# Layer 1's attention with the context: a unit's value products by key block, with TensorE's order fixed

## The chip, the cores and the metric

The kernel runs on one core of one Trainium2 chip. A core has TensorE (matrix products), VectorE, ScalarE, GpSimd and SyncE, each with its own queue of instructions, and 16 DMA engines. The metric is the device time of one execution in microseconds (us). In the profile PE is TensorE, PEld its weight loads, DVE is VectorE, ACT is ScalarE, POOL is GpSimd and SP is SyncE.

## The reference

A decoder of two layers on 8 sequences of 512 tokens of 256 numbers, all in float32, each part followed by a layer norm of its sum with its input. Layer 0: self attention with decay, attention with the context, a feed-forward part with butterfly products. Layer 1: causal self attention, attention with the context, a mixture of experts. The change is in layer 1's attention with the context, where a query attends to its own 512 tokens and to the 64 of the context (8 heads of 64 numbers):

```python
    q1 = split_heads(x1 @ Wq1, N1)
    k1 = split_heads(x1 @ Wk1, N1)
    v1 = split_heads(x1 @ Wv1, N1)
    k2 = split_heads(x2 @ Wk2, N2)
    v2 = split_heads(x2 @ Wv2, N2)
    k = jnp.concatenate([k1, k2], axis=1)
    v = jnp.concatenate([v1, v2], axis=1)
    sim = jnp.einsum('bihd,bjhd->bhij', q1.astype(jnp.float32), k.astype(jnp.float32)) * scale
    attn = jax.nn.softmax(sim, axis=-1)
    out = jnp.einsum('bhij,bjhd->bihd', attn, v)
    out = out.reshape(B, N1, h * d)
    return out @ Wo + bo
```

Then the mixture of experts normalises each token, picks two of 8 experts by a router (softmax of a product with a 256 x 8 matrix, top two), and adds their weighted outputs.

## The kernel before

The kernel is one program of phases. Each phase is a list of units that go through the stages of a software pipeline (`_pipeline`): in step s, stage k works on unit s - k, and at the end of a step one piece of a list of postponed work (`put_off`) is run. A planner then sets the order of each engine's instructions: it takes them in the program's order as priority and lets one that is ready by its own estimate go ahead of one that isn't. It also adds the waits between engines.

In the phase "l1_context" a unit is (b, c, i): sequence b (8), head pair c (4), block i of 128 queries (4). So there are 128 steps, and "a unit's" four blocks i of one (b, c) share queries, keys and values. The stages are:

- `l1x_pre`, when i is 0: products for queries and keys of all 512 tokens (L953, tile s_qk), values (L960, t_v, kept in vc, two buffers); for a new b also the transposes of x and the context's values (L941, vx).
- `l1x_scores`, a step later: for each of the two heads j, one product with the 512 own keys (L980) and one with the 64 of the context (L981), both into one PSUM tile s_sc; VectorE takes the negated maximum (L982), ScalarE the exponential with its sum (L983); then the reciprocal of the sums (L840) and the scaling (L842).
- an empty stage.
- `l1x_transposes`: for each head four transposes of 128 x 128 (L279, tile tP) and a copy to SBUF (pt); then two transposes for the context's 64 keys (L995) and their copy (pt2). Copies alternate between VectorE (L94) and ScalarE (L96).
- `l1x_values`: for the 128 queries of block i, eight products (key block k, head j) of 64 output rows and 128 columns (L1007), and two with the context's values (L1016), all into 128 columns of the PSUM tile o_pv. After the last i the tile is copied to aT; after the last c the output projection (L225, o_out, in two pieces) and the norm go to `put_off`, and after them the router's four pieces: `route_norm`, `route_transposes` (L1075), `route_picks` (L1090 and some 20 small VectorE operations), `route_places` (L1129 to L1133, then eight scatters from GpSimd's queue).

PSUM holds two score tiles of two banks (s), two tiles for transposes (t) and two for outputs (o). A ring of eight 8 KB slots in SBUF holds weights; the phase uses four of them. The next phase, the experts, begins once all tokens are routed.

A product of float32 is issued as two matmul instructions, each with its weight load.

Of the kernel before, what the change touches and what calls it, by code (L numbers as in the profile page):

```python
# [11 lines left out]
F32 = mybir.dt.float32  # L12
# [6 lines left out]
P = 128  # L19
S = 512  # L20
D = 256
S2 = 64
NT = S // P
KC = D // P
NEG = -1.0e30
LN_EPS = 1e-5
SLOT = 2048
BLK = 256


def _pipeline(units, stages, later=None):


    units = list(units)
    for step in range(len(units) + len(stages) - 1):
        for k, stage in enumerate(stages):
            if 0 <= step - k < len(units):
                stage(*units[step - k])
        if later:
            later.pop(0)()  # L40
    while later:
        later.pop(0)()

# [2 lines left out]
def decoder_kernel(ctx: ExitStack, tc: tile.TileContext, a: dict, out: bass.AP):  # L46
# [8 lines left out]
    pe, act, dve, pool, sp = nc.tensor, nc.scalar, nc.vector, nc.gpsimd, nc.sync  # L55
# [34 lines left out]
    def evac(dst, src):  # L90

        n_evac[0] += 1
        if n_evac[0] % 2:
            dve.tensor_copy(dst, src)  # L94
        else:
            act.copy(dst, src)  # L96
# [18 lines left out]
    xs = [const.tile([P, NT, D], F32, name=f"x{b}") for b in range(NB)]  # L115
# [76 lines left out]
    def normed(dst, r, on_act=False):  # L192
# [52 lines left out]
    def pt_tile():  # L245
        return ph.tile([P, 2, NT, P], F32, tag="pt", name="pt")
# [27 lines left out]
    def probs_transposed(p, pt, n):  # L274

        for j in range(2):
            t = t_tile("tP")
            for k in range(n):
                pe.transpose(t[:, k, :], p[:, j, k * P : (k + 1) * P], ident)  # L279
            evac(pt[:, j, 0:n, :], t[:, 0:n, :])  # L280


    def butterfly_ops(bfly, bias_row, ahead=4):
# [58 lines left out]
    live = {}  # L342
# [191 lines left out]
    with tc.tile_pool(name="bfly", bufs=1, side="right") as bfly, phase("l0_self") as ph, psum("a", 3, 1, 1):  # L534
# [24 lines left out]
        units = [(b, g) for b in range(NB) for g in range(4)]  # L559
        later = []  # L560
# [43 lines left out]
        o = o_tile("o_bias")  # L604
# [14 lines left out]
    woT1 = slot("woT1").rearrange("p (c n) -> p c n", c=8)  # L619
# [107 lines left out]
    def big_tile(name, bufs=1):  # L727
        return ph.tile([P, 8, S], F32, tag="big", name=name, bufs=bufs)
# [115 lines left out]
    put_off = []  # L844
# [18 lines left out]

    def l1_transposes(b, c, i):
        pt = pt_tile()
        probs_transposed(live.pop(("p", b, c, i)), pt, i + 1)
# [8 lines left out]
    def out_done(b, c, w, n, plus, then=None):  # L875
        if c == 0:
            live["aT", b] = big_tile("aT")
        aT = live["aT", b]
        evac(aT[:, c, :], live.pop(("o", b, c)))
        if c == n - 1:  # L880
            project_and_norm(b, aT, w, n, plus(), put_off)
            if then:
                then(b)

    def l1_values(b, c, i):
        pt = live.pop(("pt", b, c, i))
        _, _, v = live["qkv", b, c]
        o = out_tile(b, c, i)
        for k in range(i + 1):
            for j in range(2):  # L890
                pe.matmul(  # L891
                    o[64 * j : 64 * (j + 1)],
                    lhsT=v[:, k, 64 * j : 64 * (j + 1)],
                    rhs=pt[:, j, k, :],
                    start=(k == 0),
                    stop=(k == i),
                )
        if i == NT - 1:
            out_done(b, c, woT1, 8, lambda: xs[b])

    with phase("l1_self") as ph:
        _pipeline(
# [14 lines left out]
    wo1 = v2_o[:, 1024:2048].rearrange("p (c n) -> p c n", c=4)  # L917
    for dst, name in ((wk2, "xa_wk2"), (wv2, "xa_wv2"), (wq1, "xa_wq1"), (wk1, "xa_wk1"), (wv1, "xa_wv1"), (wo1, "xa_wo")):
        sp.dma_start(out=dst, in_=rows(a[name]))
    NC2 = NB * S2  # L920
    k2 = slot("k2").rearrange("p (c n) -> p c n", c=4)
    for c in range(4):
        o = o_tile("o_k2")
        for kc in range(KC):
            pe.matmul(
                o[:, 0:NC2],
                lhsT=wk2[:, kc, c * P : (c + 1) * P],
                rhs=ctxT[:, kc, :],
                start=(kc == 0),
                stop=(kc == KC - 1),  # L930
            )
        evac(k2[:, c, 0:NC2], o[:, 0:NC2])

    def l1x_pre(b, c, i):
        if i:
            return
        if c == 0:
            xT = x_transposed(b)
            o = o_tile("o_v2")
            for kc in range(KC):  # L940
                pe.matmul(  # L941
                    o[0:S2, :], lhsT=ctxT[:, kc, b * S2 : (b + 1) * S2], rhs=wv2[:, kc, :], start=(kc == 0), stop=(kc == KC - 1)
                )
            vx = work.tile([P, S], F32, tag="lat", name="vx")
            evac(vx[0:S2, :], o[0:S2, :])
            live["xT", b], live["vx", b] = xT, vx
        xT = live["xT", b]
        cols = slice(c * P, (c + 1) * P)
        q, k = qk_tiles()
        s = s_tile("s_qk")  # L950
        for j, w in enumerate((wq1, wk1)):
            for kc in range(KC):
                pe.matmul(s[:, j, :], lhsT=w[:, kc, cols], rhs=xT[:, kc, :], start=(kc == 0), stop=(kc == KC - 1))  # L953

        act.mul(q, s[:, 0, :], 0.125)
        dve.tensor_copy(k, s[:, 1, :])
        t = t_tile("t_v")
        for j in range(NT):
            for kc in range(KC):
                pe.matmul(  # L960
                    t[:, j, :],
                    lhsT=xT[:, kc, j * P : (j + 1) * P],
                    rhs=wv1[:, kc, cols],
                    start=(kc == 0),
                    stop=(kc == KC - 1),
                )
        v = ph.tile([P, NT, P], F32, tag="vc", name="vc")
        act.copy(v, t)
        live["qkv", b, c] = q, k, v

# [16 lines left out]
        live["p", b, c, i] = p  # L987

    def l1x_transposes(b, c, i):
        p = live.pop(("p", b, c, i))  # L990
        pt = pt_tile()
        probs_transposed(p, pt, NT)
        t = t_tile("tP2")
        for j in range(2):
            pe.transpose(t[0:S2, j, :], p[:, j, S : S + S2], ident)  # L995
        pt2 = ph.tile([P, 2, P], F32, tag="pt2", name="pt2")
        evac(pt2[0:S2], t[0:S2, 0:2, :])
        live["pt", b, c, i] = pt, pt2

    def l1x_values(b, c, i):  # L1000
        pt, pt2 = live.pop(("pt", b, c, i))
        _, _, v = live["qkv", b, c]
        vx = live["vx", b]
        o = out_tile(b, c, i)
        for k in range(NT):
            for j in range(2):
                pe.matmul(  # L1007
                    o[64 * j : 64 * (j + 1)],
                    lhsT=v[:, k, 64 * j : 64 * (j + 1)],
                    rhs=pt[:, j, k, :],  # L1010
                    start=(k == 0),
                    stop=False,
                )
        for j in range(2):
            h = c * P + 64 * j
            pe.matmul(o[64 * j : 64 * (j + 1)], lhsT=vx[0:S2, h : h + 64], rhs=pt2[0:S2, j, :], start=False, stop=True)  # L1016
# [6 lines left out]
        if i == NT - 1:  # L1023
            out_done(b, c, wo1, 4, plus, routed)


    gb = keep.tile([P, 2, KC], F32, name="gb")
# [134 lines left out]

    ph = ctx.enter_context(phase("l1_experts"))
# [135 lines left out]
    for b in range(NB):  # L1299
        t = ph.tile([P, NT, D], F32, tag="last", name="last", bufs=4)  # L1300
# [95 lines left out]
```

## Time and profile before

| | |
|---|---|
| three runs | 4045.73, 4053.77, 4060.9 us; median 4053.77 |
| the profiled execution | 4058.26 us, its span 4056.5 us, mean granted clock 0.947 |
| 0 to 971 us | layer 0's self attention |
| 971 to 1412 us | layer 0's attention with the context, its feed-forward part, and the start of layer 1 |
| 1412 to 2417 us | layer 1's self attention |
| 2417 to 3385 us | layer 1's attention with the context, router pieces between |
| 3385 to 3442 us | the last sequence's projection, norm and routing |
| 3442 to 4056.5 us | the experts and the last norm |

The stages are read from the timeline; their borders overlap by a few us. Busy times count the union of an engine's instructions; the end of a matmul in the trace is modelled, so intervals between starts say more than durations. "Idle before" is the time an engine stood still ahead of an instruction, and the name behind the arrow is what ended it.

### The profile page before, as it was taken

The page shows a single profiled execution, that of the slowest core. Times are in us where ns is not written, and L with a number is a line of the kernel's source. Part 1 is how long each engine was busy: PE and PEld are TensorE (multiplying, and loading weights), DVE is VectorE, ACT ScalarE, POOL GpSimd, SP SyncE. Part 2 cuts the span into 40 slices and gives each one's busy share as a digit, 9 for nine tenths or more (in the row PEclk, how much of TensorE's full clock was granted, in tenths as well). Part 3 has the DMA queues.
Part 4 walks back from the last instruction along what each step waited for, and adds up shares of the span by engine and source line. Part 5 has one row for each costly group of instructions (what it writes and reads, how often), then busy time and mean ns, then how long its engine had stood idle before and what let it go on. Part 6 is the DMA issues. An engine that isn't in the chain of part 4 may idle for free. (4 is left out here: it accounts for less than half of the span.)

```text
span 4056.5 us, 58011 instructions
## 1 busy us (share of the span) xinstructions
PE 3799.6 (94%) x22164; PEld 2393.7 (59%) x22164; DVE 2195.0 (54%) x6177; ACT 1418.2 (35%) x2980; POOL 1098.8 (27%) x974
## 2 busy tenths in 40 slices
PE   8999999998999999999999999999999995999995
PEld 3333333346656655666566665666666664888884
DVE  5666656558942377777777765555555553000002
ACT  2443343442221254444544433333333331222222
POOL 4767566652211122211211110110101101122222
PEclk8999899997789999999999999999999997999997
DMA  3000011119500122222322220000000001766664
GB/s 120 25 22 22 22 32 32 32 52 236 124 6 1 32 37 32 32 32 32 40 35 32 32 32 1 17 13 10 12 17 17 17 11 40 243 183 182 182 183 107
DMA packets 173432, 236.12 MB, mean 58 GB/s; under 512 B 26554, under 2 KB 138618, under 8 KB 173155
## 3 DMA queue, kind: packets, MB, share of 16 engines
q1 hardware_dynamic: 146562, 179.93, 14.6%
q0 software_dynamic: 26592, 52.49, 9.0%
q8 instruction: 175, 2.87, 0.3%
q14 instruction: 103, 0.84, 0.1%
HBM read 136.78 MB, written 62.03 MB: 49 GB/s over the span
## 5 line engine op out<-in xcount | busy, mean ns | idle before, releaser
L417 DVE CUSTOM_DVE_ANT_0 scored<-s_sc,decay 128x512 f32<-128x512 f32 x512 | 323.4, 687 | 293.4 <-PE s_sc L412 291.9
L470 ACT ACTIVATE pt<-s_st 128x1024 f32<-128x1024 f32 x256 | 261.4, 1024 | 373.0 <-PE o_pv L481 224.9
L810 POOL DMA_DIRECT2D qk<-turned x256 | 202.6, 1207 | 627.0 <-issue 273.0
L96 ACT COPY pt<-tP 128x128 f32<-128x128 f32 (+2 forms) x480 | 224.3, 467 | 384.2 <-PE tP L279 299.2
L279 PE MATMUL tP<-ident,p 128*128 128x128 f32 x2304 | 355.5, 287 | 2.3 <-DVE pt L94 0.8
L279 PEld LDWEIGHTS tP<-ident,p 128*128 128x128 f32 x2304 | 250.6, 143 | 145.8 <-issue 74.0
L269 ACT ACTIVATE p<-p,nm 128x128 f32<-128x128 f32 (+3 forms) x512 | 283.0, 555 | 145.4 <-DVE nm L267 145.4
L983 ACT ACTIVATE p<-s_sc,nm 128x576 f32<-128x576 f32 x256 | 189.6, 743 | 348.9 <-DVE nm L982 348.9
L1287 DVE TENSOR_SCALAR y<-o_y,share 128x256 f32<-128x256 f32 x78 | 34.2, 479 | 491.8 <-PE o_y L1265 491.8
L842 DVE TENSOR_SCALAR p<-p,rsum 128x576 f32<-128x576 f32 (+4 forms) x768 | 295.4, 428 | 6.1
L1249 PE MATMUL s_h<-xnT,we 128*128 128x256 f32 x1248 | 284.7, 381 | 2.8 <-DMA we<-in_mo_w 2.8
L412 PE MATMUL s_sc<-k,q 32*128 32x512 f32 x1024 | 267.5, 703 | 16.4 <-ACT k L398 14.0
L94 DVE COPY pt<-tP 128x128 f32<-128x128 f32 (+2 forms) x480 | 259.1, 540 | 42.5 <-PE tP L279 28.6
L257 DVE CUSTOM_DVE_ANT_0 p<-s_sc,tabs 128x128 f32<-128x128 f32 (+3 forms) x512 | 234.9, 484 | 84.9 <-PE s_sc L855 84.9
L855 PE MATMUL s_sc<-qk 64*128 64x128 f32 (+3 forms) x1024 | 265.8, 486 | 12.3 <-DVE turned L807 8.2
L1265 PE MATMUL o_y<-we,h 128*128 128x256 f32 x1248 | 275.6, 379 | 0.0
L1265 PEld LDWEIGHTS o_y<-we,h 128*128 128x128 f32 x1248 | 237.1, 190 | 32.2
L1249 PEld LDWEIGHTS s_h<-xnT,we 128*128 128x128 f32 x1248 | 232.6, 191 | 32.2 <-DMA we<-in_mo_w 3.2
L982 DVE TENSOR_REDUCE nm<-s_sc 128x1 f32<-128x576 f32 x256 | 183.6, 749 | 119.1 <-PE s_sc L981 119.1
L1288 POOL DMA_INDIRECT total<-y,to x78 | 121.2, 1554 | 458.5 <-DVE y L1287 295.1
L891 PE MATMUL o_pv<-pt,vc 128*64 128x128 f32 x2560 | 221.8, 284 | 0.0
L1007 PE MATMUL o_pv<-pt,vc 128*64 128x128 f32 x2048 | 197.7, 287 | 0.0
(248 smaller groups left out, 6476.1 us busy)
## 6 DMA issues: line engine op xcount, KB each, us to landing
we<-in_mo_w SPq DMA_DIRECT2D x78, 1024.0 KB, 5.7
rows_in<-zero SPq DMA_DIRECT2D x64, 530.0 KB, 11.2
qk<-turned POOLq DMA_DIRECT2D x256, 128.0 KB, 4.4
xr<-rows_in SPq DMA_DIRECT2D x39, 265.0 KB, 6.2
coef<-in_ff_upw SPq DMA_DIRECT2D x40, 256.0 KB, 3.2
coef<-in_ff_dnw SPq DMA_DIRECT2D x40, 256.0 KB, 3.1
x<-in_x SPq DMA_DIRECT2D x8, 512.0 KB, 9.4
total<-x SPq DMA_DIRECT2D x8, 512.0 KB, 2.9
```

The lines of the kernel that those rows point to most:

```text
L94: dve.tensor_copy(dst, src)
L96: act.copy(dst, src)
L257: dve.tensor_tensor_reduce(out=p[:, j, 0:n], in0=s[:, j, 0:n], in1=m, scale=1.0, scalar=-3.0e38, op0=op, op1=reduced, accum_out=mx[:, j : ...
L269: act.activation(p[:, j, 0:n], p[:, j, 0:n], AF.Exp, bias=nm[:, j : j + 1], scale=scale, accum_out=sums[:, at + j : at + j + 1],)
L279: pe.transpose(t[:, k, :], p[:, j, k * P : (k + 1) * P], ident)
L412: pe.matmul(s[:, j, :], lhsT=q[h : h + 32, i * P : (i + 1) * P], rhs=k[h : h + 32, :], start=True, stop=True)
L417: dve.tensor_tensor_reduce(out=scored[:, h, :], in0=s[:, j, :], in1=decay[:, i, :], scale=1.0, scalar=-3.0e38, op0=ALU.mult, op1=ALU.max, ...
L470: act.activation(pt, s, AF.Exp, scale=1.0 / 16.0)
L842: dve.tensor_scalar(p[:, j, 0:n], p[:, j, 0:n], rsum[:, j : j + 1], None, ALU.mult)
L855: pe.matmul(s[:, j, 0:n], lhsT=q[h : h + 64, i * P : (i + 1) * P], rhs=k[h : h + 64, 0:n], start=True, stop=True)
L1249: pe.matmul(s[:, j, :], lhsT=w1[:, c, f * P : (f + 1) * P], rhs=xnT[:, c, :], start=(c == 0), stop=(c == KC - 1),)
L1265: pe.matmul(o[:, i, :], lhsT=h[:, f, i * P : (i + 1) * P], rhs=w2[:, f, :], start=(f == 0), stop=(f == 7),)
```

## The change

Stages now carry their own delay, and they are listed in the order in which a step issues them: `l1x_pre` (0), `l1x_scores` (1), `l1x_transposes` (3), `l1x_values` (7), `l1x_last_transposes` (3). The probabilities of all four query blocks of a unit are collected transposed in two SBUF tiles of 512 columns, one for each head, in two sets by the parity of c. While the transposes of the next unit run, `l1x_values` makes one product over all 512 queries for one key block k and each head in each of four steps, and in the fourth also the two products of the context. The context's transposes stand behind the values. Within the phase TensorE takes its instructions in the program's order. Each router piece has an empty step ahead of it. vc has three buffers.

```diff
-def _pipeline(units, stages, later=None):
+def _pipeline(units, stages, later=None, pieces=1):
...
     units = list(units)
-    for step in range(len(units) + len(stages) - 1):
-        for k, stage in enumerate(stages):
+    stages = [s if isinstance(s, tuple) else (k, s) for k, s in enumerate(stages)]
+    for step in range(len(units) + max(k for k, _ in stages)):
+        for k, stage in stages:
             if 0 <= step - k < len(units):
                 stage(*units[step - k])
-        if later:
-            later.pop(0)()
+        for _ in range(pieces):
+            if later:
+                later.pop(0)()
...
-            evac(pt[:, j, 0:n, :], t[:, 0:n, :])
+            evac(pt[j], t[:, 0:n, :])
...
+    pts = [[slot("pt").rearrange("p (k n) -> p k n", k=NT) for _ in range(2)] for _ in range(2)]
...
-        v = ph.tile([P, NT, P], F32, tag="vc", name="vc")
+        v = ph.tile([P, NT, P], F32, tag="vc", name="vc", bufs=3)
...
     def l1x_transposes(b, c, i):
+        p = live["p", b, c, i]
+        if i == 0:
+            live["pt", b, c] = pts[c % 2], ph.tile([P, 2, S], F32, tag="pt2", name="pt2")
+        pt, _ = live["pt", b, c]
+        probs_transposed(p, [pt[j][:, :, i * P : (i + 1) * P] for j in range(2)], NT)
+
+    def l1x_last_transposes(b, c, i):
+
         p = live.pop(("p", b, c, i))
-        pt = pt_tile()
-        probs_transposed(p, pt, NT)
+        _, pt2 = live["pt", b, c]
         t = t_tile("tP2")
         for j in range(2):
             pe.transpose(t[0:S2, j, :], p[:, j, S : S + S2], ident)
-        pt2 = ph.tile([P, 2, P], F32, tag="pt2", name="pt2")
-        evac(pt2[0:S2], t[0:S2, 0:2, :])
-        live["pt", b, c, i] = pt, pt2
-
-    def l1x_values(b, c, i):
-        pt, pt2 = live.pop(("pt", b, c, i))
+        evac(pt2[0:S2, :, i * P : (i + 1) * P], t[0:S2, 0:2, :])
+
+    def l1x_values(b, c, k):
+
+        if k == 0:
+            live["o", b, c] = o_tile("o_pv")
+        o = live["o", b, c]
+        pt, pt2 = live["pt", b, c]
         _, _, v = live["qkv", b, c]
         vx = live["vx", b]
-        o = out_tile(b, c, i)
-        for k in range(NT):
-            for j in range(2):
-                pe.matmul(
-                    o[64 * j : 64 * (j + 1)],
-                    lhsT=v[:, k, 64 * j : 64 * (j + 1)],
-                    rhs=pt[:, j, k, :],
-                    start=(k == 0),
-                    stop=False,
-                )
+        for j in range(2):
+            pe.matmul(
+                o[64 * j : 64 * (j + 1)], lhsT=v[:, k, 64 * j : 64 * (j + 1)], rhs=pt[j][:, k, :], start=(k == 0), stop=False
+            )
+        if k < NT - 1:
+            return
         for j in range(2):
             h = c * P + 64 * j
             pe.matmul(o[64 * j : 64 * (j + 1)], lhsT=vx[0:S2, h : h + 64], rhs=pt2[0:S2, j, :], start=False, stop=True)
...
     def routed(b):
-        put_off.extend(partial(f, b) for f in (route_norm, route_transposes, route_picks, route_places))
-
-    with phase("l1_context") as ph:
+
+        for f in (route_norm, route_transposes, route_picks, route_places):
+            put_off.extend((nothing, partial(f, b)))
+
+    with phase("l1_context") as ph, tc.manual_schedule(engines={PE}):
         _pipeline(
             [(b, c, i) for b in range(NB) for c in range(4) for i in range(NT)],
-            [l1x_pre, l1x_scores, nothing, l1x_transposes, l1x_values],
+            [(0, l1x_pre), (1, l1x_scores), (3, l1x_transposes), (7, l1x_values), (3, l1x_last_transposes)],
             put_off,
         )
```

More of the change, by code (lines that the diff above doesn't have):

```diff
@@ L26 @@
 LN_EPS = 1e-5
+PE = mybir.EngineType.PE
 SLOT = 2048
 BLK = 256
-def _pipeline(units, stages, later=None):
+def _pipeline(units, stages, later=None, pieces=1):
     units = list(units)
-    for step in range(len(units) + len(stages) - 1):
-        for k, stage in enumerate(stages):
+    stages = [s if isinstance(s, tuple) else (k, s) for k, s in enumerate(stages)]
+    for step in range(len(units) + max(k for k, _ in stages)):
+        for k, stage in stages:
             if 0 <= step - k < len(units):
                 stage(*units[step - k])
-        if later:
-            later.pop(0)()
+        for _ in range(pieces):
+            if later:
+                later.pop(0)()
     while later:
@@ L865, in l1_transposes @@
         pt = pt_tile()
-        probs_transposed(live.pop(("p", b, c, i)), pt, i + 1)
+        probs_transposed(live.pop(("p", b, c, i)), [pt[:, j, 0 : i + 1, :] for j in range(2)], i + 1)
         live["pt", b, c, i] = pt
@@ L873, in out_tile, with out_done @@
         return live["o", b, c][:, i * P : (i + 1) * P]
-    def out_done(b, c, w, n, plus, then=None):
+    def out_done(b, c, o, w, n, plus, then=None):
         if c == 0:
@@ L878, in out_done @@
         aT = live["aT", b]
-        evac(aT[:, c, :], live.pop(("o", b, c)))
+        evac(aT[:, c, :], o)
         if c == n - 1:
@@ L898, in l1_values @@
         if i == NT - 1:
-            out_done(b, c, woT1, 8, lambda: xs[b])
+            out_done(b, c, live.pop(("o", b, c)), woT1, 8, lambda: xs[b])
     with phase("l1_self") as ph:
@@ L1021, in plus @@
             return xb
-        if i == NT - 1:
-            out_done(b, c, wo1, 4, plus, routed)
+        out_done(b, c, o, wo1, 4, plus, routed)
     gb = keep.tile([P, 2, KC], F32, name="gb")
```

## The prediction

> **What bounds the kernel now.** I read the page first, then the busy time by stage, then the timeline of one steady step of the changed stage, TensorE alone and then the engines that empty PSUM.
>
> ```profile
> PE 3799.6 (94%) x22164; PEld 2393.7 (59%) x22164; DVE 2195.0 (54%) x6177; ACT 1418.2 (35%) x2980; POOL 1098.8 (27%) x974
> ```
>
> ```profile
> core 0: us, PE busy (x) PEld busy (x) DVE busy (x) ACT busy (x) POOL busy (x), PEclk, DMA share, GB/s
> ...
> 2417.00:3385.00 968.00, 909.33 (x6329) 608.94 (x6327) 551.89 (x1302) 345.22 (x818) 84.43 (x77) 0.96 0.04 13
> ```
>
> The changed stage runs from 2417 to 3385 us. TensorE is busy 94% of it, VectorE 57%, ScalarE 36%, and DMA hardly at all. A unit (batch b, head pair c) has four steps, so there are 128 steps. A plain step takes 4.69 or 4.98 us by turns, mean 4.835. This is one of the longer ones, on TensorE:
>
> ```profile
> 2905.18 1.14 PE L980 MATMUL s_sc<-k,q 64*128 64x512 f32 x4
> 2906.14 0.34 PE L981 MATMUL s_sc<-k,q 64*128 64x64 f32 x4
> 2906.41 1.09 PE L279 MATMUL tP<-ident,p 128*128 128x128 f32 x8
> 2907.43 0.65 PE L1007 MATMUL o_pv<-pt,vc 128*64 128x128 f32 x6
> 2908.65 0.41 PE L995 MATMUL tP<-ident,p 128*64 128x128 f32 x2 [0.57 <-ACT pt L96]
> 2908.99 0.87 PE L1007 MATMUL o_pv<-pt,vc 128*64 128x128 f32 x10
> 2909.79 0.43 PE L1016 MATMUL o_pv<-pt,vx 64*64 64x128 f32 x4
> 2910.16 1.14 PE L980 MATMUL s_sc<-k,q 64*128 64x512 f32 x4
> ```
>
> From start to start: scores 1.23, transposes 1.02, values 1.22 (with the idle 0.57), the context's transposes 0.34, values 0.80, the context's values 0.37: 4.98. The other kind of step idles 0.27 in the same place. So a step has 4.41 us of work and 0.42 of idle time on average. The idle time ends with a copy out of PSUM, since there are only two transpose buffers and a step needs three. The engines that make those copies:
>
> ```profile
> 2906.50 1.42 DVE L982 TENSOR_REDUCE nm<-s_sc 128x1 f32<-128x576 f32 x2 [0.83 <-PE s_sc L981]
> 2907.30 0.74 ACT L983 ACTIVATE p<-s_sc,nm 128x576 f32<-128x576 f32 x1 [2.66 <-DVE nm L982]
> ...
> 2907.84 0.68 DVE L94 COPY pt<-tP 128x512 f32<-128x512 f32 x1
> ...
> 2908.03 0.58 ACT L96 COPY pt<-tP 128x512 f32<-128x512 f32 x1
> 2908.49 0.76 ACT L983 ACTIVATE p<-s_sc,nm 128x576 f32<-128x576 f32 x1
> ...
> 2909.37 0.17 DVE L840 RECIPROCAL rsum<-sums 128x2 f32<-128x2 f32 x1 [0.84 <-ACT p L983]
> 2909.57 0.95 DVE L842 TENSOR_SCALAR p<-p,rsum 128x576 f32<-128x576 f32 x2
> ```
>
> VectorE's step is 1.42 (maxima) + 0.68 (a copy) + 0.17 + 0.95 + 0.20 (the small copy every other step) = 3.42 us. The copy at 2907.84 stands behind both maxima.
>
> The change's price depends on whether products of different columns of the array run abreast when they are 512 wide. The stage itself has them only 128 wide, so I looked at layer 0, and for one undivided product at L953:
>
> ```profile
> 804.68 1.07 PE L481 MATMUL o_pv<-pt,vaug 128*32 128x512 f32 x8
> 805.68 0.73 PE L412 MATMUL s_sc<-k,q 32*128 32x512 f32 x4
> ...
> 2890.09 3.70 PE L953 MATMUL s_qk<-xT,q_k 128*128 128x512 f32 x8
> 2893.62 1.95 PE L960 MATMUL t_v<-v_k,xT 128*128 128x128 f32 x16
> ```
>
> Every float32 product is issued as two instructions. Undivided ones take 0.44 us each at 512 columns (3.53/8). The eight of L481, four column tiles by two, take 1.00 us to the next group's start, so four run abreast.
>
> **What the Trainium skill says.** "TensorEngine Tiling", Key Properties: tiles work in parallel, and changing the tiling mode drains TensorE. The trace agrees: four abreast above, and 1.00 us where two passes alone are 0.88. "TensorE: Matmul & The Clock Gate", Part 1 (engine queue depths): VectorE and ScalarE take their queues in strict order; the copy behind the maxima shows it. The same part says that TensorE's clock halves after idle windows. The trace has a mean of 0.96 here, with dips after the router's 8-wide products; these stay.
>
> **The change, part by part.**
>
> *Values.* Before, a step's 8 value products (16 instructions) are cut by the planner as 10 and 6 or 6 and 10, an odd number of products each, so that one of each part runs unpaired. Work: (1.22 - 0.57) + 0.80 = 1.45, and 0.37 for the context, 1.82 a step. After, a step has two products of 512 columns, one pair abreast: 1.00 us as L481, its mode change included. Each unit's fourth step adds the context pair, 1.00 again. Columns streamed are equal; what goes is the unpaired slots and mode changes. Not shown is a pair of 64 columns at 512. Bounds: 1.00 (abreast), 0.88 + 0.88 + 0.10 = 1.86 (one after the other). I take 1.00, since 64-column pairs at 128 columns and 32-column groups at 512 both run abreast.
>
> *Work of a step after.* 1.23 + 1.02 + 1.00 + 0.34 = 3.59, in the fourth 4.59; mean 3.84, against 4.41.
>
> *Idle time after.* TensorE's order is now scores, transposes, values, the context's transposes. I put the copies where the trace has them, counted from the end of the scores. A step whose first copy is on ScalarE: maxima 0.09 to 1.51, first exponential to 1.63, first copy to 2.20, second exponential to 2.84. One whose first copy is on VectorE: copy 1.43 to 2.11, second exponential done at 2.35, scaling to 3.62, small copy to 3.95. TensorE is ready for the third transpose at 2.02 and gets its buffer at about 2.2: idle 0.15 to 0.24. The fourth step (3.02) waits for nothing. Queued behind that wait are the next scores, and behind these both maxima. The next scores start at 2.51 to 2.6, but their second half needs the bank that the second exponential frees, in the ScalarE kind of step at about 2.96 (2.84, and 0.12 because VectorE came late from the small copy). So one kind of step takes 2.51 + 1.23 = 3.74, the other about 3.0 + 1.23 = 4.25; mean 4.0, fourth step 4.6; over a unit 4.15. VectorE's 3.42 fits, with 0.7 to spare where it had 1.4.
> Gain: (4.835 - 4.15) x 128 = 88 us.
>
> *Start and end.* Values run three steps further behind. At the end four value groups and the context's stand alone (5.0 us) where one step's stood (about 1.5): +3.5. At the start three more steps run without values, at VectorE's pace rather than TensorE's; and the first transposes can't be drawn ahead of the stage (six of eight are at 2405.8 now): about +1.5. Together -5.
>
> *Router pieces.* The same instructions, with an empty step before each, three steps later in the batch. VectorE's normalisation and picks come to about 14 us a batch, TensorE's products to 6.5. SP's store and POOL's eight scatters move along; only the last batch's are waited for, in the tail from 3385 to 3442, which stays. The fixed order adds a real wait: the transposes (L1075), L1090 and L1129 stand in TensorE's queue, and everything behind them waits for VectorE. In the unloaded tail the normalisation takes 8 us (3392.3 to 3400.4) and the picks 4.3 (3406.6 to 3410.9). Loaded, there are 22 us for the first (four steps and one projection of 5.3), which mostly covers it, and 8.3 for the second, with VectorE 0.7 free in each step. Bounds: 0 and 5 us a batch; I take 1.75, 14 us in all.
>
> *At nothing.* Value buffers taken from the ring (four slots that only the next stage needs, after 3442), a third vc buffer, wider pt2: no engine time. The copies have the same sizes, with another stride.
>
> Sum: 88 - 5 - 14 = 69 us. The profiled execution took 4058.3 (span 4056.5); 4058.3 - 69 = 3989. The runs' median is 4.5 us lower, so I forecast 3985.
>
> **Rivals.**
> *TensorE alone sets the pace* (no idle time: the planner puts copies ahead of maxima where it helps): 3.84 a step, 127 - 5 = 122, 3932. For it: VectorE and ScalarE have room on average. Against: two transpose buffers and two score buffers stay.
> *The softmax loop sets it*, scores to maxima to exponential to the next scores, at about 4.45 a step because a copy falls into it: 49 - 5 - 20, 4030. For it: the second exponential is already behind a copy in half of the steps.
> *TensorE held at the router, slower*: the fixed order keeps scores behind L1075, L1090 and L1129, whose inputs VectorE delivers late since it is now 85% busy in a plain step. It decides from (88 - 5)/8 = 10.4 us of waiting a batch. At 13 us, 4075. Against: the 22 us of lead.
> *The pair doesn't run abreast*: steps of 4.45, fourth 6.31, mean 4.92: +11 + 5 + 14, 4084.
>
> **How the numbers follow.** About 0.5% (20 us) can be told from no change. My forecast 0.58 (its own range 3955 to 4015), TensorE alone 0.14, softmax loop 0.14, held at the router 0.10, not abreast 0.04. Half of the softmax loop's falls within 0.5%, and a little of the router's. Faster 0.79, same 0.08, slower 0.13. The range takes in the first rival and the softmax loop's upper side: 3935 to 4050.
>
> **What would show it.** Right: value products of 512 columns starting in pairs a few ns apart, a group about 1.0 us; plain steps near 4.0 and 4.6; idle time before L995's transposes down from 0.42 to about 0.15; the stage some 70 us shorter. Wrong: values at 1.8 us a group; idle time of several us before L1075, L1090 or L1129; scores waiting for the exponential in every step; or a clock well under 0.96 in the stage.

## The result, and the profile after

The changed kernel takes 3995.78 us (median of 4 runs, 3987.99 to 3997.32) against 4052.96 us of the kernel before: ratio 0.985, 95% interval 0.9833 to 0.9868. The forecast was 3985 us, 0.3% lower. The profiled execution took 3987.99 us, the shortest of the four, with a span of 3986.3 us where the kernel before had 4056.5. So the two traces differ by 70 us, the medians by 57.

First the busy times and the two stages, from the page and from the view of busy time by stretch (columns as in the prediction; the first row is layer 1's attention with the context, the second the last sequence's projection and routing):

```profile
PE 3727.7 (94%) x20244; PEld 2264.5 (57%) x20244; DVE 2191.8 (55%) x6177; ACT 1418.0 (36%) x2980; POOL 1097.8 (28%) x974
```

```profile
2412.00:3313.00 901.00, 845.32 (x4407) 489.68 (x4405) 551.89 (x1301) 345.92 (x818) 81.09 (x74) 0.96 0.04 13
3313.00:3379.00 66.00, 21.04 (x91) 17.84 (x90) 18.56 (x85) 4.61 (x7) 13.42 (x14) 0.59 0.17 60
```

TensorE has 1920 instructions fewer, which is 128 steps times 15. The stage has shrunk from 968 to 901 us, and of these 67 us 64 are TensorE's busy time (909.33 to 845.32). VectorE's busy time in it is the same to 0.01 us. The tail, from the stage's last value product to the experts' first product, was 64 us before and is 66. So what was gained was gained in the stage that was changed, and as work of TensorE. The rest of the 70 us of the span is 5.5 us by which the stage begins earlier, in phases that the change doesn't touch (in the traces of this study it begins anywhere between 2407 and 2423 us).

The timeline of TensorE, two steps (start, duration, engine, line, operation, tiles, shapes, count; then the idle time before and what ended it):

```profile
2882.05 0.41 PE L1008 MATMUL tP<-ident,p 128*64 128x128 f32 x2 [0.20 <-ACT pt L100]
2882.39 1.52 PE L986 MATMUL s_sc<-k,q 64*128 64x512 f32 x4
2883.35 0.72 PE L987 MATMUL s_sc<-k,q 64*128 64x64 f32 x4
2884.00 1.09 PE L283 MATMUL tP<-ident,p 128*128 128x128 f32 x8
2885.02 1.08 PE L1020 MATMUL o_pv<-pt,vc 128*64 128x512 f32 x4
2886.03 0.41 PE L1008 MATMUL tP<-ident,p 128*64 128x128 f32 x2
2886.37 1.14 PE L986 MATMUL s_sc<-k,q 64*128 64x512 f32 x4
2887.33 0.34 PE L987 MATMUL s_sc<-k,q 64*128 64x64 f32 x4
2887.61 1.09 PE L283 MATMUL tP<-ident,p 128*128 128x128 f32 x8
2888.63 1.08 PE L1020 MATMUL o_pv<-pt,vc 128*64 128x512 f32 x4
2889.64 1.08 PE L1027 MATMUL o_pv<-pt,vx 64*64 64x512 f32 x4
2890.64 0.41 PE L1008 MATMUL tP<-ident,p 128*64 128x128 f32 x2
```

From start to start the four instructions of L1020 take 1.01 us, and the context's (L1027) 1.00. The first step is 3.98 us; its scores take 1.61 where the second step's take 1.24, because their second half waits for a score buffer. The second step is a unit's fourth.

What TensorE waits for in the stage (engine, tile and line, what ended the wait: us in total, times, longest):

```profile
PE tP L1008 <- ACT pt L100: 21.0, 52, 1.6
PE tP L1008 <- DVE pt L98: 13.1, 11, 2.4
...
PE o_rank L1139 <- DVE both L1129: 6.1, 7, 1.2
```

and before:

```profile
PE tP L995 <- ACT pt L96: 29.5, 54, 0.6
PE tP L995 <- DVE pt L94: 21.8, 49, 3.3
```

The wait for a transpose buffer, 51.3 us before, is still the largest, with 34.1. The router's ranks hold TensorE for 6.1 us in all.

### The profile page after: what moved, and what is told of

It reads as the page before. It is cut to its first block, busy times and chain, and to the rows that moved or that the text cites. A ratio compares the mean times of both kernels' runs of the same rounds, so it can differ in the third digit from the quotient of the medians.

```text
span 3986.3 us, 54132 instructions
## 1 busy us (share of the span) xinstructions
PE 3727.7 (94%) x20244; PEld 2264.5 (57%) x20244; DVE 2191.8 (55%) x6177; ACT 1418.0 (36%) x2980; POOL 1097.8 (28%) x974
## 5 line engine op out<-in xcount | busy, mean ns | idle before, releaser
L989 ACT ACTIVATE p<-s_sc,nm 128x576 f32<-128x576 f32 x256 | 189.5, 742 | 291.5 <-DVE nm L988 253.1
L416 PE MATMUL s_sc<-k,q 32*128 32x512 f32 x1024 | 266.6, 699 | 16.4 <-ACT k L402 14.0
L895 PE MATMUL o_pv<-pt,vc 128*64 128x128 f32 x2560 | 221.8, 284 | 0.0
L1155 POOL DMA_INDIRECT rows_in<-z,irow x64 | 63.1, 985 | 475.0 <-DVE hit L1150 347.6
## 6 DMA issues: line engine op xcount, KB each, us to landing
rows_in<-zero SPq DMA_DIRECT2D x64, 530.0 KB, 10.2
```

The costliest lines, as they stand in the source:

```text
L416: pe.matmul(s[:, j, :], lhsT=q[h : h + 32, i * P : (i + 1) * P], rhs=k[h : h + 32, :], start=True, stop=True)
L989: act.activation(p[:, j, :], s[:, 0 : S + S2], AF.Exp, bias=nm[:, j : j + 1], accum_out=sums[:, j : j + 1])
```

## The experiments

All kernels compute the whole of the reference. Below, "the change" is the changed kernel, "narrow" values are those of the kernel before (128 columns, ten small products a step), "wide" ones those of the change. Ratios are to the kernel before in the same session, with their 95% interval.

**Part one: which part of the change brings the gain.** Four variants of the change, each with one part undone. In the first the planner orders TensorE again:

```diff
-    with phase("l1_context") as ph, tc.manual_schedule(engines={PE}):
+    with phase("l1_context") as ph:
```

> The changed kernel, with TensorE's order in this phase left to the planner again. Theory A (the gain is in the step's work: whole pairs and fewer mode changes): in this shape the planner's order differs from the program's in few places, mostly at the start and beside the router, so 3985 to 4005 us. Theory B (the fixed order brings the gain): back near 4050.

Measured: 3987.9 us, 0.9824 (0.9806 to 0.9842); the stage is 901.2 us long, the change's 900.8. Fixing the order brings nothing. (TensorE stands idle for 33.7 us in it instead of 55.7, but its scores take 207.1 us from start to start instead of 194.3: where one head's half of the scores waits while the other's runs, TensorE isn't idle.)

In the second the router's pieces come in successive steps, as before the change:

```diff
-            put_off.extend((nothing, partial(f, b)))
+            put_off.append(partial(f, b))
```

> The changed kernel, with the router's pieces in successive steps, without the empty step ahead of each. Theory A, as in the prediction: with TensorE's order fixed, TensorE meets the router's products before VectorE has made their inputs, about 4 us more of waiting a batch at the normalised tokens' transposes and at the rank products: 4020 to 4040. Rival (VectorE catches up in any case, the empty steps do nothing): 3990 to 4000.

Measured: 4037.05 us, 0.9947 (0.9933 to 0.9961): two thirds of the gain are gone. The views of waits and of busy time by stretch of this kernel:

```profile
PE o_rank L1139 <- DVE both L1129: 19.8, 7, 3.1
```

```profile
2460.00:3340.00 880.00, 815.34 (x4110) 476.86 (x4108) 519.40 (x1222) 321.01 (x758) 80.83 (x73) 0.92 0.04 13
```

and the change's own row over about as much work (4171 matmul instructions against 4110):

```profile
2460.00:3300.00 840.00, 790.35 (x4171) 460.37 (x4168) 520.81 (x1235) 324.89 (x772) 75.74 (x68) 0.96 0.04 13
```

The wait for the picks is 19.8 us instead of 6.1, a mean of 2.8 over seven batches instead of 0.9. More is lost in another way: the stage is 54 us longer (955.2 to 900.8, by the starts on TensorE), its idle time only 18 (74.0 to 55.7). The other 36 are work at a lower clock: 0.92 in the stretch instead of 0.96. The trace's record of the granted clock, which has only full and half speed in this stage, gives 157 us at half speed against 75; idle time left out, that costs some 38 us. The empty steps are therefore worth two things, a shorter wait and a higher clock.

In the third the values are narrow again, one step after the transposes, with the fixed order, the context's transposes still behind the values and the router still apart (vc has two buffers again):

```diff
-            [(0, l1x_pre), (1, l1x_scores), (3, l1x_transposes), (7, l1x_values), (3, l1x_last_transposes)],
+            [(0, l1x_pre), (1, l1x_scores), (3, l1x_transposes), (4, l1x_values), (3, l1x_last_transposes)],
...
     def l1x_transposes(b, c, i):
+        pt = pt_tile()
+        probs_transposed(live["p", b, c, i], pt, NT)
+        live["pt", b, c, i] = pt
...
+    def l1x_values(b, c, i):
+        pt, pt2 = live.pop(("pt", b, c, i))
```

> The values in the old shape (eight products of 128 columns and two of the context for one block of queries, one step after the transposes), but with TensorE's order fixed, the context's transposes behind the values, and the router's pieces apart. Theory A (whole pairs, and the third transpose's wait covered by the values): work 1.23 + 1.02 + 1.03 + 0.37 + 0.34 = 3.99 us a step, mean about 4.06 with idle time, so 3975 to 4000, no slower than the wide form. Theory C (the 512-wide products themselves bring it): 4030 to 4055.

Measured: 3964.25 us, 0.977 (0.9754 to 0.9787). This was the surprise of the study: without the wide products the kernel is about 0.8% *faster* than with them. Its timeline of one step, and two of its groups (instructions, busy us, mean ns, idle before):

```profile
2896.21 1.09 PE L281 MATMUL tP<-ident,p 128*128 128x128 f32 x8
2897.23 1.09 PE L1013 MATMUL o_pv<-pt,vc 128*64 128x128 f32 x16
2898.26 0.44 PE L1022 MATMUL o_pv<-pt,vx 64*64 64x128 f32 x4
2898.62 0.41 PE L1001 MATMUL tP<-ident,p 128*64 128x128 f32 x2
```

```profile
L1013 PE MATMUL o_pv<-pt,vc 128*64 128x128 f32 x1920 | 135.3, 285 | 0.0
...
L1001 PE MATMUL tP<-ident,p 128*64 128x128 f32 x238 | 48.6, 286 | 16.0 <-ACT pt L98 9.6 <-DVE pt L96 6.3
```

against the change's:

```profile
L1020 PE MATMUL o_pv<-pt,vc 128*64 128x512 f32 x484 | 132.2, 625 | 0.0
...
L1008 PE MATMUL tP<-ident,p 128*64 128x128 f32 x242 | 49.6, 287 | 31.9 <-ACT pt L100 18.8 <-DVE pt L98 12.0
```

The sixteen small instructions stand together and take 1.03 us, the four large ones 1.01. So the 1.45 us that a step's own values cost before weren't the price of small products: it was that of products cut by the planner into parts of ten and six instructions, five and three products, each with one that has no partner.

The starts of the single instructions in the two traces say what this costs. Two that run abreast start 6 or 7 ns apart, and the next pair, or the next that is alone, 109 ns later. Sixteen together are eight pairs. Of ten, eight are paired and two alone, of six, four are paired and two alone: ten slots for eight, 0.22 us. From start to start the parts take 0.80 and 0.58 us, 1.38 in all (the other 0.07 of the 1.45 is already the wait). So 0.14 us of the difference to 1.03 is left for the second change of kind. In the stage before, 508 of the 2048 instructions start alone, here none.

The narrow form has 0.36 us of the context's values in every step, the wide one 1.00 in every fourth.

In the fourth the values are wide, but the two products of a step belong to the same head, so that neither has a partner on the other half of the columns:

```diff
-        for j in range(2):
+        j = k // 2
+        for kk in (2 * (k % 2), 2 * (k % 2) + 1):
             pe.matmul(
-                o[64 * j : 64 * (j + 1)], lhsT=v[:, k, 64 * j : 64 * (j + 1)], rhs=pt[j][:, k, :], start=(k == 0), stop=False
+                o[64 * j : 64 * (j + 1)], lhsT=v[:, kk, 64 * j : 64 * (j + 1)], rhs=pt[j][:, kk, :], start=(kk == 0), stop=False
             )
```

> The changed kernel, but the two products of a step belong to one head (two key blocks of head 0 in the first and second step, of head 1 in the third and fourth), so the same columns of the array and no pair; the number and size of products is unchanged. Theory A (pairs run abreast): a group takes 1.86 instead of 1.00 us, the wait for the third transpose goes, +0.55 us a step, 4055 to 4075. Theory C (width is what counts): 3990 to 4000.

Measured: 4035.6 us, 0.9949 (0.9936 to 0.9963), some 40 us more than the change. Its timeline:

```profile
2892.11 1.93 PE L1021 MATMUL o_pv<-pt,vc 128*64 128x512 f32 x4
2893.97 0.41 PE L1008 MATMUL tP<-ident,p 128*64 128x128 f32 x2
```

The group takes 1.86 us, the upper bound of the prediction, and 0.85 us more than a pair: 109 us over 128 steps. Only 40 of these show, since the longer group covers waits: only 2.9 us of idle time follow the values here (31.9 in the change), and the scores, whose second half no longer waits, take 181.5 us in the stage instead of 194.3.

**Part two: where the narrow form's gain comes from.** Three more kernels: narrow values as in the third above but with the planner's order; the same with the fixed order and the context's transposes ahead of the values; and the kernel before with an empty step ahead of each router piece, nothing else changed.

```diff
-    with phase("l1_context") as ph, tc.manual_schedule(engines={PE}):
+    with phase("l1_context") as ph:
```

> The kernel of e3 (narrow values, the context's transposes behind them, router pieces apart) with TensorE's order left to the planner. Theory A (what counts is the order in which the program lists the work, and that pairs stay whole; the fixing itself is not needed where the planner keeps that order): 3955 to 3985. Theory B (the fixed order itself): 4030 or more.

Measured: 3966.37 us, 0.9769 (0.9755 to 0.9784).

```diff
-            [(0, l1x_pre), (1, l1x_scores), (3, l1x_transposes), (4, l1x_values), (3, l1x_last_transposes)],
+            [(0, l1x_pre), (1, l1x_scores), (3, l1x_transposes), (3, l1x_last_transposes), (4, l1x_values)],
```

> The kernel of e3 with one thing moved: the context's transposes ahead of the values, as the kernel before lists them, in the fixed order. Theory A: the third transpose waits for the first copy, about 1.15 us after TensorE is ready, with nothing to cover it and the whole queue behind it: step 5.1 against 4.06, 4070 to 4105. Rival (another wait of the step shrinks by as much, so this one is hidden anyway): below 4000.

Measured: 4106.91 us, 1.0113 (1.0097 to 1.0128), slower than the kernel before. The timeline shows why:

```profile
2895.84 1.09 PE L281 MATMUL tP<-ident,p 128*128 128x128 f32 x8
2898.09 0.41 PE L1001 MATMUL tP<-ident,p 128*64 128x128 f32 x2 [1.16 <-ACT pt L98]
2898.43 0.77 PE L1013 MATMUL o_pv<-pt,vc 128*64 128x128 f32 x10
```

The third pair of transposes needs the buffer of the first, whose copy comes about 2.2 us after the transposes began. With nothing between them TensorE stands 1.16 us here, 135 us in the stage; with the values between, nothing in the step shown above and 16 us in the stage. The planner of the kernel before got around this by putting ten or six of the sixteen instructions between, and paid with the unpaired ones. So this one place in the list, behind or ahead of the values, decides whether TensorE waits, or the values are cut, or neither.

```diff
-        put_off.extend(partial(f, b) for f in (route_norm, route_transposes, route_picks, route_places))
+        for f in (route_norm, route_transposes, route_picks, route_places):
+            put_off.extend((nothing, partial(f, b)))
```

> The kernel before with the router's pieces apart and nothing else changed. Theory A: with the planner's order TensorE didn't wait at the router before, so the empty steps bring nothing by themselves: 4040 to 4065. Rival (part of the gain is the router's): 4000 to 4035.

Measured: 4035.53 us, 0.994 (0.9921 to 0.9959). That is at the border of the two ranges. Spreading the router is worth 0.6% on the kernel before alone, although TensorE waited for none of its pieces there. Its stage (columns as before):

```profile
2423.00:3372.00 949.00, 899.11 (x6328) 608.36 (x6326) 548.80 (x1302) 345.17 (x818) 84.84 (x77) 0.96 0.04 13
```

It is 19 us shorter than before. Of these, 9 are idle time (58.7 to 49.9), and the clock has little to do with it here: 75 us of half speed instead of 82, worth some 3 us. The rest of the gain was not traced to a place.

Two more complete the table: narrow values, the context's transposes last and the router in successive steps, once in the fixed order and once in the planner's. The second of them is the kernel before with nothing but the third transposes listed behind the values.

```diff
-            put_off.extend((nothing, partial(f, b)))
+            put_off.append(partial(f, b))
```

> The kernel of e3 with the router's pieces in successive steps, order fixed. Theory A (in a fixed order TensorE reaches the rank products before VectorE has the picks, idles, and its clock is halved): 3990 to 4010, some 25 to 45 us above e3. Rival (only the wide form suffers): 3960 to 3972.

> The kernel before with one thing changed: the context's transposes are listed behind the values, so that the planner, which orders everything, takes them there. Theory A (most of the gain is whole pairs and a covered wait, and the planner can shift the router's products): 3965 to 3995. Rival (needs the router pieces apart as well, planner or not): 4000 to 4020.

Measured: 4003.77 us, 0.9873 (0.9849 to 0.9896), and 4000.41 us, 0.9858 (0.9834 to 0.9881). The first is as slow as theory A has it, but TensorE waits in another place, for the normalised tokens and not for the picks:

```profile
PE tZ L1081 <- DVE z L211: 21.4, 7, 3.1
```

The second falls to the rival: the router has to be apart with the planner's order too. Even so the one line listed elsewhere brings as much as the whole change (0.9858 and 0.985).

| ratio to the kernel before | router in successive steps | router apart |
|---|---|---|
| narrow, third transposes early, planner (before) | 1 | 0.9940 |
| narrow, third transposes early, fixed | not run | 1.0113 |
| narrow, third transposes last, planner | 0.9858 | 0.9769 |
| narrow, third transposes last, fixed | 0.9873 | 0.9770 |
| wide, third transposes last, planner | not run | 0.9824 |
| wide, third transposes last, fixed | 0.9947 | 0.9850 (the change) |

Read down: with the planner the transposes' place brings 1.4 to 1.7%, wide products take back 0.5 to 0.8%. The fixed order costs 1.7% where the third transposes are early, and with them last changes the time by no more than 0.3%, and not for the better. Read across: the router apart brings 0.6 to 1.0%.

**Part three: the wait that the wide form leaves.** Since three of four wide steps have too little between the first and the third transposes, I gave the third a bank of its own, out of the two for outputs, and in another kernel also fixed the engines of the copies, the first on VectorE and the others on ScalarE.

```diff
-        t = t_tile("tP2")
+        t = o_tile("tP2").rearrange("p (i n) -> p i n", n=P)
```

> The changed kernel, with the context's transposes in one of the two output banks and not in a transpose bank, so that they needn't wait for the first copy. Theory A (the 35 us of idle time ahead of them in the changed kernel is a wait for a bank): 3960 to 3980. Rival (the next scores then wait for their own bank instead): 3985 to 4000.

Measured: 4006.06 us, 0.9863 (0.9847 to 0.9878), no better than the change and above both ranges. Some of its waits, and one step:

```profile
PE o_rank L1139 <- DVE pt L98: 6.3, 3, 2.2
...
PE s_qk L959 <- ACT p L989: 6.0, 6, 1.2
PE o_out L229 <- ACT pt L100: 4.3, 7, 0.8
PE o_r L1100 <- DVE pt L98: 4.0, 3, 1.3
...
PE tP L1008 <- DVE pt L98: 2.3, 3, 1.1
```

```profile
2888.82 1.36 PE L986 MATMUL s_sc<-k,q 64*128 64x512 f32 x3
...
2890.02 0.59 PE L986 MATMUL s_sc<-k,q 64*128 64x512 f32 x1
...
2890.71 1.09 PE L283 MATMUL tP<-ident,p 128*128 128x128 f32 x8
```

The wait before L1008 is gone as meant, but each of its parts has a successor. Projections, the router's product and its ranks now wait for the output banks, which the small copies hold. And the scores, which begin earlier, run into the wait for the exponential: what follows them starts at 2890.71, 1.89 us after their start, where a step that doesn't wait has 1.24. In the stage the scores take 211.9 us instead of 194.3.

```diff
-        probs_transposed(p, [pt[j][:, :, i * P : (i + 1) * P] for j in range(2)], NT)
+        for j, copy in ((0, dve.tensor_copy), (1, act.copy)):
+            t = t_tile("tP")
+            for k in range(NT):
+                pe.transpose(t[:, k, :], p[:, j, k * P : (k + 1) * P], ident)
+            copy(pt[j][:, :, i * P : (i + 1) * P], t)
...
-        evac(pt2[0:S2, :, i * P : (i + 1) * P], t[0:S2, 0:2, :])
+        act.copy(pt2[0:S2, :, i * P : (i + 1) * P], t[0:S2, 0:2, :])
```

> f8, and the copies no longer alternate: the first always on VectorE, the second and third on ScalarE behind both exponentials. Theory A (in every other step the second exponential stands behind a copy and holds the next scores' second half): plain steps 3.6 to 3.75, fourth steps 4.6, 3940 to 3962. Rival (VectorE's 3.2 us chain sets the step): as f8, 3965 to 3980.

Measured: 3999.82 us, 0.9855 (0.9837 to 0.9874), above both ranges too. My theory that some 0.2 us a step could be had by freeing that buffer fell in both: behind a short wait on one bank there were others on the next.

**Part four: further apart.** With two empty steps ahead of each piece, on the best kernel so far:

```diff
-            put_off.extend((nothing, partial(f, b)))
+            put_off.extend((nothing, nothing, partial(f, b)))
```

> The kernel of e3 with two empty steps ahead of each router piece. Theory A (one empty step already lets VectorE finish each piece before TensorE needs it; what is left of halved clock follows the 8-wide products themselves): 3955 to 3968. Rival (the gain goes on with the distance): 3925 to 3950.

Measured: 3985.37 us, 0.980 (0.977 to 0.983). It isn't faster than with one step (0.977), which neither theory had; the intervals overlap, but the stage in the trace is longer, 889.2 us against 873.3. A wait of VectorE in this kernel, in the one with one empty step, and in the one with successive steps and the planner's order:

```profile
DVE z L1127 <- DMA rows_in<-z,irow: 35.8, 6, 8.1
```

```profile
DVE z L1127 <- DMA rows_in<-z,irow: 25.6, 7, 5.3
```

```profile
DVE z L1127 <- DMA rows_in<-z,irow: 36.7, 7, 6.5
```

L1127 copies token numbers into the rows to be scattered, and has to wait until the scatters of the previous batch have read them. VectorE, which takes its queue in order, stands up to 8.1 us with maxima and copies behind that instruction. On this line VectorE loses 10 us more than with one empty step. It loses as much with successive steps, so the distance by itself doesn't set this wait. Of the 16 us by which the stage is longer, TensorE's idle time is 5 (31.9 against 26.8), and 82 us at half speed instead of 68 are another 5 to 7; the rest I didn't trace.

The best version is thus the narrow one with the third transposes last and the router apart, 3964 to 3966 us in either order: 2.3% faster than before.

## Why the prediction was right, and where its reasons were not

The table compares TensorE's time in the stage, worked out from the traces: the sum of intervals from one start to the next, from the context's key products to the stage's last value product; an interval holds the wait that follows.

| us | before | the change | narrow, third last, apart |
|---|---|---|---|
| values and the context's values | 290.0 | 200.2 | 199.8 |
| scores | 180.7 | 194.3 | 186.9 |
| transposes, all three | 182.1 | 191.7 | 183.8 |
| start of a batch (tT, o_v) | 23.2 | 35.3 | 28.2 |
| the rest | 291.5 | 279.3 | 274.6 |
| stage | 967.5 | 900.8 | 873.3 |
| of this, idle | 58.7 | 55.7 | 26.8 |

*Right.* The sum of the parts, 69 us, met 66.7 in the stage. A step was right: of the steps without other work the 58 plain ones have a median of 3.96 us and the 23 fourth ones 4.73, over a unit 4.15 as forecast. A pair of 64 columns at 512, taken as 1.00, took 1.01; its upper bound, 1.86, is what the group takes when both products use the same columns. The idle time of 0.20 before L1008 at 2882.05 lies within the forecast 0.15 to 0.24, and the fourth step waits for nothing. The step whose scores wait for the second exponential exists; it takes 3.98 us rather than 4.25, as their second half was late by 0.37 and not by 0.5. The fourth takes 4.6 to 5.0 in 21 of the 23.

*Luck.* The 88 us of the steps less the 66.7 of the stage leave 21, where the deductions came to 19, but made up of other things: 6.1 and not 14 at the router, and two items that the sum hadn't, 12 for the first products of the batches and 6.3 for scores that wait for keys copied by VectorE. By the medians the gain is 57 us. And it hangs on the router's empty steps, which the sum had as part of a cost: without them 21 us are left (0.9947).

*The cause of the gain in the values.* The prediction put it to "the unpaired slots and mode changes". Both are shown, by the 1.03 us of the sixteen narrow instructions that stand together and by their starts; the width isn't needed. What the prediction missed is that the place of the context's transposes behind the values, which it used only to put the wait, does this by itself: 1.4% with no other change. With narrow values in one piece the first row of the table falls by 90 us. Of these 35 are the wait (51.3 to 16.4); by the starts, an estimate, 254 slots of 109 ns are 28 us, and 134 groups of values fewer, at 0.14 us, are 19; 8 are left over.

The wide form still has less work for TensorE, 128 x 1.01 + 32 x 1.00 = 161 us against 128 x (1.03 + 0.36) = 178. It loses this again ahead of the context's transposes, 34.1 us of idle time against 16.4, because it puts the context's product in one step of four: three of four have 1.01 us between the second transposes and the third, which with the 1.02 of the transposes is 2.03 us ahead of a buffer that comes at about 2.2; the narrow form has 1.39, so 2.41. So the first row is equal. The 27.5 us by which the stage is longer lie in the other rows: 7.4 in the scores, 7.9 in the transposes (6.1 of it the wait for the ranks), 7.1 at the start of a batch. This says where the time is and not why the wide form is slower, which no run shows: with the planner's order its wait ahead of the third transposes is 20.7 us, in part three 3.4, and neither kernel is clearly faster than the change.

*The size of the idle time.* "Idle time before L995's transposes down from 0.42 to about 0.15" came out at 34.1 / 128 = 0.27. The plain waits were sized rightly, but not the few long ones: the 11 that VectorE's copy ended have a mean of 1.19 us. One of them, on TensorE, and what VectorE did then:

```profile
2871.26 0.41 PE L1008 MATMUL tP<-ident,p 128*64 128x128 f32 x2 [1.87 <-DVE pt L98]
```

```profile
2869.11 0.17 DVE L1131 COPY z<-tokens_at 128x4 f32<-128x4 f32 x1 [2.44 <-DMA rows_in<-z,irow]
2869.19 1.41 DVE L988 TENSOR_REDUCE nm<-s_sc 128x1 f32<-128x576 f32 x2
2870.52 0.68 DVE L98 COPY pt<-tP 128x512 f32<-128x512 f32 x1
```

The copy of token numbers again (L1131 here). It waits for the scatters of the batch before, and with it wait the maxima and the copy that frees TensorE's buffer. The prediction said of the scatters that "only the last batch's are waited for"; that was wrong, and the waits of VectorE before (16.2 us on this line) showed it.

*The router.* The wait was taken as 1.75 us a batch, 14 in all; it came to 6.1 for the ranks. (There are 3.0 us ahead of the transposes of the normalised tokens too, but 2.5 of them end with a copy out of a transpose buffer and not with the normalisation.) That the pieces apart were worth 0.6% on their own wasn't in the sum at all: they were costed as an addition. The prediction's "these stay", of the clock's dips, held (82 us at half speed before, 75 in the change), but only with the pieces apart: in successive steps it was 157, and the prediction had no term for that. "TensorE: Matmul & The Clock Gate", Part 1, says that idle windows halve the clock, and the page bears on this more than I used it: here dips follow the router's narrow products and the waits beside them, so where these are placed matters.

*The start.* For the start of the stage the sum had 1.5 us, which no trace singles out. Not in it was that the first products of the batches take 12 us more in the stage. The values, three steps later, end a unit later, and so the ranks' products now come right ahead of the next batch's first products:

```profile
3183.49 1.85 PE L1143 MATMUL o_rank<-both,ones 128*128 128x8 f32 x8
3185.20 1.95 PE L188 MATMUL tT<-ident,x 128*128 128x128 f32 x8
3187.07 2.87 PE L947 MATMUL o_v<-v_o,ctxT 128*64 128x512 f32 x4
```

Before, the eight transposes took 1.09 us and the four products 1.93. The granted clock from 3183 to 3190 us is 0.57, and 1.00 from 3195 on. In the narrow kernel the dip falls on a step of scores instead, so part of these 12 us is paid there elsewhere.

*Rivals.* TensorE alone was not reached, since buffers and banks took over from each other (part three). The softmax loop is seen in some steps, as one wait among others. The router held TensorE for 6.1 us, and where its pieces stood close for about 20, not the 83 that would have made the change slower. "Not abreast" was refuted by the 1.01 us, and its price, 4084, isn't what the kernel with unpaired values has to be held against: it had the context's products unpaired too, 0.86 x 32 = 28 us, which that kernel leaves paired. That makes 4056; measured were 4035.6, and the 20 us between them were not traced.

Open remain why the wide form is slower, a third of the router's gain on the kernel before, part of the longer stage with two empty steps, and the few us by which the planner's order was better than the fixed one for wide values: the intervals of 0.9824 and 0.985 overlap.

## What to carry to other kernels

Where products of half the array run in pairs, count how many stand together: an odd number between two changes of kind leaves one without a partner (here 0.11 us for each odd part), every further change of kind costs as well (here 0.14 us), and one instruction that waits for a buffer, placed in their middle, can make both parts odd; put it behind the longest run of work that doesn't need the buffer. Compare what covers a wait with that wait step by step, not on the average: a product that is bundled into one step of four leaves the other three short. When a change has several parts, try each on the kernel before: here two small ones, a line's place in a list and an empty step between pieces, gave 2.3%, and the large one gave some of it back.

## What the runs showed of the hardware that I had not expected

Products on different rows of the array don't keep the order of the queue. In the change each head issues its own product (L986) and then that of the context (L987), first for one head and then for the other, and in this phase TensorE takes its instructions in the program's order. The trace has all four instructions of L986 first, at 2886.37, and those of L987 from 2887.33; the first starts of the two heads are 14 ns apart, so the second head's product goes ahead of the first head's L987 by about 0.95 us. (The trace shows the starts; the queue is read from the program.) "TensorE: Matmul & The Clock Gate", Part 3 ("What overlaps and what doesn't"), says that matmuls start and end strictly in order. In this trace their starts don't, for row halves that are used by two independent chains; whether the ends do can't be said, as ends are modelled there.

Narrow products bring TensorE's clock down, and no wait is needed for it. In the kernel with narrow values, the third transposes last and the router apart, the ranks' products of eight columns begin without any idle time ahead of them, and from 2927.7 to 2931.1 us TensorE has half its clock, through scores that had nothing to do with them:

```profile
2926.55 1.04 PE L1139 MATMUL o_rank<-both,ones 128*128 128x8 f32 x8
2927.51 1.97 PE L982 MATMUL s_sc<-k,q 64*128 64x512 f32 x4
...
2933.13 1.14 PE L982 MATMUL s_sc<-k,q 64*128 64x512 f32 x4
```

Of the fifteen stretches at half speed in this stage, each of 3.4, 6.8 or 10.2 us, eleven begin within 4.5 us of router products with no idle time in between, and the other four after 1.6 to 3.4 us of idle time. In the change the ranks stand behind a wait of up to 1.2 us and are followed by 3.4 or 6.8 us at half speed; with waits of 2.8 us a batch (the router in successive steps) the mean clock of the stage fell from 0.96 to 0.92.
